# Two graph layers on one core: transposes of the norms through VectorE and DRAM, output products spread over two steps

## The chip, the cores and the metric

The kernel runs on one core of a Trainium2 chip. A core has five engines that run side by side, each through its own instructions in order: TensorE (matmuls; PE in the profile, with its weight loads as PEld), VectorE (DVE), ScalarE (ACT), GpSimd (POOL) and SyncE (SP), which here only issues the transfers (DMA) between DRAM and the on-chip memory SBUF. TensorE writes its results into PSUM[...]. The metric is the device time of one execution in microseconds.

## The reference, cut to what matters

x holds 64 batches of 256 rows of 512 float32 values; `adj` is one 256x256 mask for all. Two layers, each on a normalised and clipped copy of x:

```python
# layer 0: one head; W is 512x256, a is 2x256
h = relu(layernorm(x)) @ W
e = leaky_relu(h @ a[0] + (h @ a[1]).T, 0.2) + NEG * (1 - adj)
x = x + concat([softmax(e) @ h, h])
# layer 1: 8 heads of 64
n = relu(layernorm(x))
q, k, v = n @ Wq.T + bq, n @ Wk.T + bk, n @ Wv.T + bv
attn = softmax(where(adj == 0, -inf, q @ k.T / 8))      # for each head
x = x + (attn @ v) @ Wo.T + bo
```

## The kernel before

The batches are taken in 32 groups of two (`GB = 2`; `GT = 4` tiles of 128 rows in a group). Three groups are under way at once. While the attention of group g runs (four **steps**: two batches, each in two `quad`s of four heads), the q, k, v products of group g+1 (`project`, 21 pieces) and the first layer of group g+2 (`first_layer`) are cut into pieces and strung between. Each product with a 512x512 weight is done by a scheme with seven half-size products in place of eight (`seven`, `operand_sums`), which needs sums of the operand's blocks first.

A matmul needs the normalised x with its columns on the partitions. `norm_T` normalises a tile of 128 rows on VectorE and turns it on TensorE, by four transposes of 128x128 into a PSUM bank; ScalarE clips it on the way out:

```python
def norm_T(src, mv, name):
    ve = small.tile([P, GT], F32, tag="ve", ...)
    nc.vector.tensor_scalar(ve, mv[:, :, 1], EPS, None, op0=ALU.add)
    nc.gpsimd.tensor_tensor(rstd, ve, rexp, op=ALU.pow)      # all four tiles at once
    def normed(t):
        xn[t] = att.tile([P, D], F32, tag="xn", ..., bufs=2)
        latest[0] = nc.vector.tensor_scalar(                 # line 354
            xn[t], src[:, t, :], mv[:, t, 0:1], rstd[:, t : t + 1],
            op0=ALU.subtract, op1=ALU.mult).ins.name
    def put(t, dst):
        if t + 1 < GT:
            normed(t + 1)
        pt = mm(f"pt{name}_{t}").rearrange("p (c t) -> p c t", c=HP)
        for c in range(HP):
            transpose(pt[:, c, :], xn[t][:, c * P : (c + 1) * P], ident)
        nc.scalar.activation(dst, pt, AF.Relu)
    normed(0)
    return put
```

`mm(...)` takes the next of five rotating PSUM banks, `held_bank(n, ...)` one of three fixed ones. `matmul` and `transpose` keep TensorE's instructions in the order of the program.

```python
def first_layer(g):                       # each yield ends a piece
    for t in range(GT): stats(mv, xt, t, ...)           # bn_stats, bn_aggr on VectorE
    put = norm_T(xt, mv, f"0_{g}")
    yield GAP
    ...                                   # per tile: put, then ph = hT @ W (H), x += H on GpSimd
    ...                                   # pn, e: scores of the first layer
    for r in range(GT):                   # po = e @ H, times 1/sum, added to x
        ...
        stats(mv, xt, r, f"1_{g}")
        yield
    put = norm_T(xt, mv, f"1_{g}")
    yield GAP
    for t in range(GT): put(t, hT[:, :, t * P : (t + 1) * P]); ...
    operand_sums(quads, sums)             # four GpSimd instructions
    for t in range(GT): nc.gpsimd.tensor_add(xt[:, t, :], xt[:, t, :], b_out)

def scores(g, b, quad):                   # a step's first half
    ...                                   # sc = k.T q; p = exp(sc) on ScalarE
    nc.vector.tensor_mul(pair, pair, maskT...)           # line 573
    nc.gpsimd.tensor_add(ps[...], pair[:, :, 0, :], pair[:, :, 1, :])

def weigh(g, b, quad, p, ps):             # one step later
    pr = mm(f"pr_{name}")...
    ...                                   # pr = v.T p, 16 matmuls
    total = held_bank(2, f"total_{name}")[:, :N]
    for j in range(QH):                   # sums over the rows
        matmul(total[j * S : (j + 1) * S, :], ones[:, :S], ps[:, j, :], start=True, stop=True)
    nc.vector.reciprocal(r, total)                       # line 604
    nc.vector.tensor_mul(oT[:, 2 * quad : 2 * quad + 2, :], pr, r...)

def outputs(g, b):                        # seven pieces, after a batch's second weighing
    operand_sums(quads, sums)             # four GpSimd instructions (o_sums)
    first = held_bank(2, f"py1_{g}_{b}")[:, : D // 2]
    product(first, 1, True)
    add(0, 0, first)                      # VectorE: x += product, line 628
    yield
    ...

steps = ("uosuoosuosoosuos", "uusususususu", "uosoosuosoosuos", "uusususususu")
for g in range(NG):
    for step, parts in enumerate(steps):
        if waiting is not None:
            weigh(*waiting)
            if waiting[2] == NQ - 1: late = outputs(*waiting[:2])
        waiting = (g, b, quad, *scores(g, b, quad))
        for part in parts:                # u: project(g+1), o: outputs, s: first_layer(g+2)
            ...
```

Beside it stand `last_bias`, a small product at the start whose four columns are built on VectorE in one buffer, and `judge`, some small matmuls that bound the sizes of the scores.

Of the kernel before, what the change touches and what calls it, by code (L numbers as in the profile page):

```python
# [14 lines left out]
P = 128  # L15
# [8 lines left out]
LARGEST_VALUE = 1e6  # L24

# [17 lines left out]
def bounded(  # L43
# [23 lines left out]
    nc = tc.nc  # L67
    B, N, D = x.shape
# [17 lines left out]
    psum = ctx.enter_context(tc.tile_pool(name="psum", bufs=1, space=bass.MemoryType.PSUM))  # L86

# [15 lines left out]


# [13 lines left out]
    xg = x.rearrange("(g b) (t p) d -> g p (b t) d", b=GB, p=P)  # L118
    og = out.rearrange("(g b) (t p) d -> g p (b t) d", b=GB, p=P)
# [3 lines left out]
    def load(g):  # L123
        xs[g] = big.tile([P, GT, D], F32, tag="x", name=f"x{g}", bufs=4)
        nc.sync.dma_start(xs[g], xg[g])

    load(0)
# [16 lines left out]
    for c in range(HP):  # L144
        for s in range(2):
            nc.vector.scalar_tensor_tensor(
                prod, w0_sb[:, c, 2:], 1.0, a_b[:, s, :], op0=ALU.mult, op1=ALU.mult,
                accum_out=w0_sb[:, c, s : s + 1],
            )
    edge = att.tile([P, NT, N], F32, tag="e", name="edge")  # L150
    nc.vector.tensor_scalar(edge, adj_i, 0.0, None, op0=ALU.not_equal)
# [6 lines left out]
    nc.vector.tensor_copy(maskT, pt)  # L158

    nc.vector.reduce_max(bad[:, 0, :], edge, axis=AX.X)  # L160
    nc.vector.tensor_scalar(bad[:, 0, :], bad[:, 0, :], 0.0, None, op0=ALU.is_equal)
    nc.vector.tensor_tensor(edge, edge, adj_i, op=ALU.not_equal)
    nc.vector.reduce_max(bad[:, 1, :], edge, axis=AX.X)

    load(1)
    load(2)

# [28 lines left out]
    rexp = const.tile([P, GT], F32, name="rexp")  # L196
    nc.gpsimd.memset(rexp, -0.5)
    ones = const.tile([P, P], F32, name="ones")
    nc.gpsimd.memset(ones, 1.0)

    def weight_sums(name):
        w = w_sb[name]
        first = nc.vector.tensor_sub(w[:, :, T3, :], w[:, :, W22, :], w[:, :, W12, :])
        after(first, latest[0])
        nc.vector.tensor_sub(w[:, :, T1, :], w[:, :, W12, :], w[:, :, W11, :])
        nc.vector.tensor_sub(w[:, :, T2, :], w[:, :, W22, :], w[:, :, T1, :])
        nc.vector.tensor_sub(w[:, :, T4, :], w[:, :, W21, :], w[:, :, T2, :])

    def last_bias():


        pb = mm("pb")
        for q in range(NQ):
            for half in range(2):
                b = small.tile([P, P], F32, tag="power", name=f"bv_{q}_{half}", bufs=1)
                nc.vector.tensor_scalar(b, ones, bv_col[:, half, q : q + 1], None, op0=ALU.mult)
                matmul(
                    pb, b, w_sb["o"][:, half, 2 * q : 2 * q + 2, :],
                    start=(q == 0 and half == 0), stop=(q == NQ - 1 and half == 1),
                )  # L220
        nc.vector.tensor_add(b_out, pb, b_out)


    def judge():
# [5 lines left out]
        nc.vector.memset(part, 0.0)  # L230
        junk = att.tile([P, D], F32, tag="junk", name="junk", bufs=1)

        def squares(col, *srcs):
            sums = small.tile([P, HP], F32, tag="sums", name=f"sums{col}", bufs=2)
            for i, src in enumerate(srcs):
                nc.scalar.activation(
                    junk[:, : src.free_size()], src, AF.Square, accum_out=sums[:, i : i + 1]
                )
            nc.vector.reduce_sum(part[:, col : col + 1], sums[:, : len(srcs)], axis=AX.X)

        for s in range(2):
            squares(s, w0_sb[:, :, s])
        squares(2, *[w0_sb[:, c, 2:] for c in range(HP)])
        wv = att.tile([P, HP, D // HP], F32, tag="block", name="wv_block", bufs=1)
        sums = small.tile([P, HP], F32, tag="sums", name="sums3", bufs=2)
        for c in range(HP):
            nc.sync.dma_start(
                wv, wvT[:, c * P : (c + 1) * P].rearrange("(c p) o -> p c o", p=P)
            )
            nc.scalar.activation(  # L250
                junk, wv.rearrange("p c o -> p (c o)"), AF.Square, accum_out=sums[:, c : c + 1]
            )
        nc.vector.reduce_sum(part[:, 3:4], sums, axis=AX.X)
        squares(4, bcol["q"])
        squares(5, bcol["k"])
        squares(6, bv_col.rearrange("p h q -> p (h q)"))
        nc.vector.reduce_max(part[:, 7:8], bad.rearrange("p a t -> p (a t)"), axis=AX.X)
        yield
        heads = const.tile([P, P], F32, name="heads")
        nc.vector.memset(heads, 0.0)  # L260
        for j in range(2):
            nc.vector.memset(heads[j * DH : (j + 1) * DH, j * DH : (j + 1) * DH], 1.0)
        rowsq = const.tile([P, 2, HP], F32, name="rowsq")
        for n, (name, src) in enumerate((("q", wqT), ("k", wkT))):
            for hp in range(HP):
                w = att.tile([P, HP, P], F32, tag="block", name=f"w{name}_block{hp}", bufs=1)
                nc.sync.dma_start(
                    w, src[:, hp * P : (hp + 1) * P].rearrange("(c p) o -> p c o", p=P)
                )
                yield  # L270
                gram = mm(f"gram_{name}{hp}")[:, :P]
                for c in range(HP):
                    matmul(
                        gram, w[:, c, :], w[:, c, :], start=(c == 0), stop=(c == HP - 1)
                    )
                a = small.tile([P, P], F32, tag="power", name=f"power_{name}{hp}_0", bufs=1)
                nc.vector.tensor_mul(a, gram, heads)
                yield
                for i in range(3):
                    square = mm(f"square_{name}{hp}_{i}")[:, :P]  # L280
                    matmul(square, a, a, start=True, stop=True)
                    if i < 2:
                        a = small.tile(
                            [P, P], F32, tag="power", name=f"power_{name}{hp}_{i + 1}", bufs=1
                        )
                        nc.vector.tensor_copy(a, square)
                    else:
                        nc.scalar.activation(
                            junk[:, :P], square, AF.Square, accum_out=rowsq[:, n, hp : hp + 1]
                        )  # L290
                    yield
        nc.vector.reduce_sum(part[:, 8:10], rowsq, axis=AX.X)
# [3 lines left out]
        nc.vector.tensor_scalar(norm, total, 1e-30, None, op0=ALU.add)  # L296
        power = const.tile([P, 10], F32, name="power")
        nc.gpsimd.memset(power, 0.5)
        nc.gpsimd.memset(power[:, 7:8], 1.0)
        nc.gpsimd.memset(power[:, 8:10], 1.0 / 32)  # L300
        nc.gpsimd.tensor_tensor(norm, norm, power, op=ALU.pow)
# [5 lines left out]
        nc.vector.tensor_add(test[:, 0:1], norm[:, 0:1], norm[:, 1:2])  # L307
        nc.vector.tensor_scalar(
            test[:, 0:1], test[:, 0:1], root / LARGEST_SCORE, None, op0=ALU.mult
        )  # L310
        nc.vector.tensor_scalar(side, norm[:, 8:10], root, None, op0=ALU.mult)
        nc.vector.tensor_add(side, side, norm[:, 4:6])
        nc.vector.tensor_mul(test[:, 1:2], side[:, 0:1], side[:, 1:2])
        nc.vector.tensor_scalar(
            test[:, 1:2], test[:, 1:2], scale / LARGEST_SCORE, None, op0=ALU.mult
        )
        nc.vector.tensor_scalar(
            test[:, 2:3], norm[:, 2:3], root / LARGEST_VALUE, None, op0=ALU.mult
        )
        nc.vector.scalar_tensor_tensor(  # L320
            test[:, 3:4], norm[:, 3:4], root, norm[:, 6:7], op0=ALU.mult, op1=ALU.add
        )
        nc.vector.tensor_scalar(
            test[:, 3:4], test[:, 3:4], 1.0 / LARGEST_VALUE, None, op0=ALU.mult
        )
        nc.vector.tensor_scalar(test[:, 4:5], norm[:, 7:8], 2.0, None, op0=ALU.mult)
        nc.vector.tensor_scalar(test, test, 1.0, None, op0=ALU.is_le)
        held = const.tile([P, 1], F32, name="held")
        nc.vector.tensor_reduce(held, test, axis=AX.X, op=ALU.min)
        nc.vector.tensor_scalar(wrong, held[0:1, :], -1.0, 1.0, op0=ALU.mult, op1=ALU.add)  # L330
# [5 lines left out]
    GAP = "gap"  # L336

    def stats(mv, src, t, name):
        st = small.tile([P, 6], F32, tag="st", name=f"st{name}_{t}")
        nc.vector.bn_stats(st, src[:, t, :])  # L340
        nc.vector.bn_aggr(mv[:, t, :], st)

    def norm_T(src, mv, name):


        ve = small.tile([P, GT], F32, tag="ve", name=f"ve{name}")
        nc.vector.tensor_scalar(ve, mv[:, :, 1], EPS, None, op0=ALU.add)
        rstd = small.tile([P, GT], F32, tag="rstd", name=f"rstd{name}")
        nc.gpsimd.tensor_tensor(rstd, ve, rexp, op=ALU.pow)
        xn = {}  # L350

        def normed(t):
            xn[t] = att.tile([P, D], F32, tag="xn", name=f"xn{name}_{t}", bufs=2)
            latest[0] = nc.vector.tensor_scalar(  # L354
                xn[t], src[:, t, :], mv[:, t, 0:1], rstd[:, t : t + 1],
                op0=ALU.subtract, op1=ALU.mult,
            ).ins.name

        def put(t, dst):
            if t + 1 < GT:  # L360
                normed(t + 1)
# [712 lines left out]
```

## Time and profile before

| | |
|---|---|
| time, median of three | 2699.87 us |
| profiled span | 2697.3 us |
| mean granted TensorE clock | 0.993 |
| busy: PE, DVE, ACT, POOL | 2620.4, 1669.7, 835.9, 1230.0 us |
| moved by DMA | 78.49 MB, 29 GB/s in the mean |

In the profile "L113" is the line of a helper that records every matmul, so matmuls are told apart by the tiles they write: `pq`, `pk`, `pv` projections, `sc` scores, `pr` and `total` weighing, `py` output products, `ph`, `pn`, `po` first layer, `pt` transposes of the norms. A group of instructions is shown with its busy time, the mean duration of one, and the idle time of its engine ahead of it with what ended it. Matmuls overlap one another, so the mean duration of one is more than the time between two.

### The profile page before, as it was taken

The page shows a single profiled execution, that of the slowest core. Times are in us where ns is not written, and L with a number is a line of the kernel's source. Part 1 is how long each engine was busy: PE and PEld are TensorE (multiplying, and loading weights), DVE is VectorE, ACT ScalarE, POOL GpSimd, SP SyncE. Part 2 cuts the span into 40 slices and gives each one's busy share as a digit, 9 for nine tenths or more (in the row PEclk, how much of TensorE's full clock was granted, in tenths as well). Part 3 has the DMA queues.
Part 4 walks back from the last instruction along what each step waited for, and adds up shares of the span by engine and source line. Part 5 has one row for each costly group of instructions (what it writes and reads, how often), then busy time and mean ns, then how long its engine had stood idle before and what let it go on. Part 6 is the DMA issues. An engine that isn't in the chain of part 4 may idle for free.

```text
span 2697.3 us, 41512 instructions
## 1 busy us (share of the span) xinstructions
PE 2620.4 (97%) x17150; PEld 2118.8 (79%) x17150; DVE 1669.7 (62%) x2558; ACT 835.9 (31%) x1771; POOL 1230.0 (46%) x1004
## 2 busy tenths in 40 slices
PE   5999999999999999999999999999999999999997
PEld 3888888878888887887788888788878878878874
DVE  5666566666557665566665576665576656666544
ACT  2333232333332333323333323333333333233321
POOL 2353355443445443545434454435455335445343
PEclk8999999999999999999999999999999999999998
DMA  5000101000001010000000000000000000000000
GB/s 164 1 12 32 36 24 36 13 32 32 28 32 36 9 36 32 24 32 9 32 32 24 32 32 9 32 32 24 32 32 9 32 32 24 32 17 23 17 16 25
DMA packets 45890, 78.49 MB, mean 29 GB/s; under 512 B 3712, under 2 KB 10624, under 8 KB 45696
## 3 DMA queue, kind: packets, MB, share of 16 engines
q1 hardware_dynamic: 45696, 75.77, 8.1%
q8 instruction: 137, 2.24, 0.3%
q14 instruction: 57, 0.47, 0.1%
HBM read 42.21 MB, written 33.55 MB: 28 GB/s over the span
## 4 chain that ended last, share of the span: by engine, by line
PE 89%; DVE 8%; POOL 1%; issue 1%; DMA 0%; ACT 0%; DVEq 0%
PE pq L113 15%; PE pv L113 14%; PE py L113 13%; PE pk L113 13%; PE pr L113 9%; PE ph L113 8%; PE sc L113 7%; PE po L113 4%; PE pt L116 4%; DVE p L573 3%; DVE r L604 2%; PE total L113 2%; DVE k L544 1%; DVE oT L605 1%; PE pn L116 1%
## 5 line engine op out<-in xcount | busy, mean ns | idle before, releaser
L573 DVE TENSOR_TENSOR p<-p,maskT 128x1024 f32<-128x1024 f32 x256 | 398.6, 1588 | 0.6 <-ACT p L572 0.5
L572 ACT ACTIVATE p<-sc 128x512 f32<-128x512 f32 x512 | 264.4, 602 | 380.9 <-PE sc L113 380.9
L574 POOL TENSOR_TENSOR ps<-p 128x512 f32<-128x512 f32 x256 | 366.2, 1447 | 0.0
L628 DVE TENSOR_TENSOR x<-py,x 128x256 f32<-128x256 f32 x448 | 187.6, 419 | 272.8 <-PE py L113 266.9
L604 DVE RECIPROCAL r<-total 128x256 f32<-128x256 f32 x128 | 224.5, 1754 | 194.6 <-PE total L113 194.6
L113 PE MATMUL py<-wo_sb,o_sums 128*128 128x256 f32 x1024 | 266.5, 384 | 26.4 <-DVE x L628 21.6
L420 POOL TENSOR_TENSOR x<-H,x 128x256 f32<-128x256 f32 x128 | 87.7, 685 | 443.0 <-ACT H L419 441.9
L113 PE MATMUL pr<-p,v 128*32 128x256 f32 x4096 | 251.8, 385 | 5.8 <-DVE p L573 5.8
L113 PE MATMUL sc<-q,k 64*128 64x256 f32 x2048 | 255.7, 389 | 0.0
L113 PE MATMUL pq<-sums,wq_sb 128*128 128x256 f32 x1024 | 246.7, 384 | 4.2 <-POOL sums L377 3.7
L113 PE MATMUL ph<-w_sb,hT 128*128 128x258 f32 x1024 | 246.1, 383 | 0.0
L113 PE MATMUL pk<-sums,wk_sb 128*128 128x256 f32 x1024 | 244.8, 382 | 0.0
L113 PE MATMUL pv<-wv_sb,sums 128*128 128x256 f32 x1024 | 242.0, 379 | 0.1
L113 PEld LDWEIGHTS sc<-q,k 64*128 64x128 f32 x2048 | 187.2, 186 | 69.7 <-issue 52.6
L113 PEld LDWEIGHTS py<-wo_sb,o_sums 128*128 128x128 f32 x1024 | 191.2, 192 | 62.9 <-POOL o_sums L377 37.6
L365 ACT ACTIVATE hT<-pt 128x512 f32<-128x512 f32 x256 | 153.1, 599 | 266.0 <-PE pt L116 265.7
L354 DVE TENSOR_SCALAR xn<-x,mv,rstd 128x512 f32<-128x512 f32 x256 | 225.8, 893 | 9.5 <-PE pt L116 4.9
L376 POOL TENSOR_TENSOR o_sums<-oT 128x256 f32<-128x256 f32 x64 | 106.2, 1660 | 262.6 <-DVE oT L605 262.6
L113 PEld LDWEIGHTS pq<-sums,wq_sb 128*128 128x128 f32 x1024 | 190.1, 191 | 39.1 <-issue 9.9
L113 PEld LDWEIGHTS ph<-w_sb,hT 128*128 128x128 f32 x1024 | 195.7, 192 | 28.6
L113 PEld LDWEIGHTS pk<-sums,wk_sb 128*128 128x128 f32 x1024 | 189.3, 190 | 33.9 <-issue 9.9
L113 PEld LDWEIGHTS pr<-p,v 128*32 128x32 f32 x4096 | 121.1, 110 | 112.2 <-issue 39.7
(145 smaller groups left out, 4054.4 us busy)
## 6 DMA issues: line engine op xcount, KB each, us to landing
x<-in_x_dram SPq DMA_DIRECT2D x32, 1024.0 KB, 5.5
out_dram<-x SPq DMA_DIRECT2D x64, 512.0 KB, 2.8
wq_sb<-in_L_gnn_Wq_dram SPq DMA_DIRECT2D x2, 512.0 KB, 11.7
wk_sb<-in_L_gnn_Wk_dram SPq DMA_DIRECT2D x2, 512.0 KB, 12.4
wv_sb<-in_L_gnn_Wv_dram SPq DMA_DIRECT2D x2, 512.0 KB, 11.4
wo_sb<-in_L_gnn_Wo_dram SPq DMA_DIRECT2D x8, 128.0 KB, 3.3
wv_block<-in_L_gnn_Wv_dram SPq DMA_DIRECT2D x4, 256.0 KB, 3.0
wq_block<-in_L_gnn_Wq_dram SPq DMA_DIRECT2D x4, 256.0 KB, 2.9
```

Source lines behind the costliest of these rows:

```text
L113: in_order(nc.tensor.matmul(*args, **kwargs))
L116: in_order(nc.tensor.transpose(*args))
L354: latest[0] = nc.vector.tensor_scalar(xn[t], src[:, t, :], mv[:, t, 0:1], rstd[:, t : t + 1], op0=ALU.subtract, op1=ALU.mult,).ins.name
L365: nc.scalar.activation(dst, pt, AF.Relu)
L376: nc.gpsimd.tensor_add(sums[:, 0], a21, a22)
L420: nc.gpsimd.tensor_add(xt[:, t, F1:], H[:, t, 2 : F1 + 2], xt[:, t, F1:])
L544: nc.vector.tensor_add(part(1, 1), first, p7)
L572: nc.scalar.activation(pair[:, j], sc[j], AF.Exp, scale=scale)
L573: nc.vector.tensor_mul(pair, pair, maskT[:, None, :, :].to_broadcast([P, 2, NT, N]))
L574: nc.gpsimd.tensor_add(ps[:, 2 * i : 2 * i + 2, :], pair[:, :, 0, :], pair[:, :, 1, :])
L604: nc.vector.reciprocal(r, total)
L628: nc.vector.tensor_add(to, out, to)
```

## The change

It takes the transposes of the norms off TensorE. VectorE turns the 32x32 blocks of a normalised tile; a transfer writes a batch to DRAM, and four transfers read it back so that block (j, i) comes to where block (i, j) was; ScalarE clips it on the way to its place. Only the first group is still turned on TensorE, as nothing stands beside it to hide the way through DRAM. Around this the pieces are rearranged:

- the norm of x goes one batch at a time, in pieces of its own (`n`), a step or more ahead of the first layer that uses it; x is loaded by batch;
- the output products of a batch are spread over two steps, and the sums of their operands move from GpSimd to VectorE;
- the rows' sums run ahead of the weighing, in a rotating bank;
- the addition of the last bias to x is put a step later; the columns of `last_bias` are built on GpSimd, each in a place of its own; `judge` works on the weights already in SBUF and runs at the start;
- `not_sooner` ties an instruction to the one recorded before it on its engine, so that it isn't put ahead.

```diff
+    def not_sooner(engine, operation, *args, **kwargs):
+        last = engine.last
+        after(getattr(engine, operation)(*args, **kwargs), last)
...
+    def norm_T(src, mv, name, by_pe):
+        def norm(b):
+            vector.tensor_scalar(ve, mv[:, tiles, 1], EPS, None, op0=ALU.add)
+            gpsimd.tensor_tensor(rstd, ve, rexp, op=ALU.pow)
+            for t in range(NT):
+                xn[r] = att.tile([P, D], F32, tag="xn", ..., bufs=2)
+                not_sooner(vector, "tensor_scalar", xn[r], src[r], mv[:, r, 0:1], rstd[:, t : t + 1],
+                    op0=ALU.subtract, op1=ALU.mult)
+        def turn(b):
+            if by_pe:
+                ...                       # as before, on TensorE
+                return
+            xt = att.tile([P, J, HP, NT, S], F32, tag="xt", ..., bufs=1)
+            moved = att.tile([P, J, HP, NT, S], F32, tag="moved", ...)
+            passed = dram.tile([P, J, HP * NT * S], F32, tag="passed", ...)
+            for t in tiles:
+                not_sooner(vector, "transpose",
+                    xt[:, :, :, t % NT, :], xn[t].rearrange("p (c j a) -> p j c a", j=J, a=S))
+                turned[t] = moved[:, :, :, t % NT, :].rearrange("p i c n -> p c i n")
+            nc.sync.dma_start(passed, xt.rearrange("p j c t n -> p j (c t n)"))
+            for j in range(J):
+                nc.sync.dma_start(
+                    moved[j * S : (j + 1) * S].rearrange("a i c t n -> a i (c t n)"),
+                    passed.rearrange("(i a) j e -> j a i e", a=S)[j])
+        def put(b, dst):
+            ...                           # two relus on ScalarE, by not_sooner
...
+    def first_norm(g):                    # six pieces: norm, turn, norm, turn, put, put
...
             stats(mv, xt, r, f"1_{g}")
+            if r == 2:
+                norm(0)
+            elif r == 3:
+                turn(0)
             yield
+        norm(1)
+        yield
+        turn(1)
+        yield
+        put(0, hT[:, :, :N])
+        yield
+        put(1, hT[:, :, N:])
...
+        total = mm(f"total_{name}")[:, :N]
+        ...                               # total and its reciprocal, now ahead of pr
         pr = mm(f"pr_{name}").rearrange("p (h n) -> p h n", h=2)
-        total = held_bank(2, f"total_{name}")[:, :N]
...
+        if quad == NQ - 1:
+            operand_sums(vector, quads, sums)
...
-    steps = ("uosuoosuosoosuos", "uusususususu", "uosoosuosoosuos", "uusususususu")
+    steps = ("Suuunuonuonuuo", "Sssnuosuosouso", "Sususuososuos", "sSsuuousouounuonsu")
...                                       # S: scores, n: a piece of first_norm(g+2), later (g+3)
+            if step == 0 and g + 1 < NG:
+                residual(g + 1)           # x += b_out
```

## The prediction

> **What bounds the kernel now.** I read four views in this order: busy time by engine with the chain that ended last, the waits of the matmul engine, its busy time by stretch, and the costliest groups.
>
> ```profile
> PE 2620.4 (97%) x17150; PEld 2118.8 (79%) x17150; DVE 1669.7 (62%) x2558; ACT 835.9 (31%) x1771; POOL 1230.0 (46%) x1004
> ...
> PE 89%; DVE 8%; POOL 1%; issue 1%; DMA 0%; ACT 0%; DVEq 0%
> ```
>
> PE is busy for 97% of the span and makes up 89% of the chain. So almost every microsecond on PE is a microsecond of the result, and the other engines matter only where PE waits for them. The waits of PE between 140 and 2494 us are few:
>
> ```profile
> PE py L113 <- DVE x L628: 19.9, 25, 1.0
> PE pt L116 <- DVE xn L354: 2.9, 1, 2.9
> PE py L113 <- DVE part L292: 0.6, 1, 0.6
> ```
>
> The columns are the total, the count and the longest. PE's only repeated wait is for VectorE to add an output product into x: 25 times about 0.8 us. By stretch, the first, a long middle and the last (the columns are length, then PE, PEld, DVE, ACT, POOL busy):
>
> ```profile
> 0.00:67.50 67.50, 35.86 (x129) 25.51 (x130) 38.23 (x93) 17.21 (x44) 18.73 (x28) 0.87 0.51 164
> ...
> 202.50:1300.00 1097.50, 1087.86 (x7184) 885.69 (x7182) 678.73 (x1050) 346.05 (x736) 506.15 (x410) 1.00 0.08 29
> ...
> 2630.00:2697.30 67.30, 49.85 (x365) 33.56 (x363) 33.54 (x41) 8.85 (x17) 25.00 (x19) 0.88 0.07 25
> ```
>
> PE idles 31.6 us at the start, 17.5 us at the end, and 9.6 us in 1097 us of the middle. In the timeline one group of two batches (from the first scores matmul of one to that of the next, 1263.1 to 1344.6) takes 81.5 us, with PE busy for 80.65. The groups that the change touches:
>
> ```profile
> L116 PE MATMUL pt<-ident,xn 128*128 128x128 f32 x1024 | 156.2, 276 | 10.6 <-DVE xn L354 10.6
> ...
> L573 DVE TENSOR_TENSOR p<-p,maskT 128x1024 f32<-128x1024 f32 x256 | 398.6, 1588 | 0.6 <-ACT p L572 0.5
> L354 DVE TENSOR_SCALAR xn<-x,mv,rstd 128x512 f32<-128x512 f32 x256 | 225.8, 893 | 9.5 <-PE pt L116 4.9 <-POOL rstd L349 3.6 <-issue 0.2
> L604 DVE RECIPROCAL r<-total 128x256 f32<-128x256 f32 x128 | 224.5, 1754 | 194.6 <-PE total L113 194.6
> ...
> L376 POOL TENSOR_TENSOR o_sums<-oT 128x256 f32<-128x256 f32 x64 | 106.2, 1660 | 262.6 <-DVE oT L605 262.6
> L349 POOL TENSOR_TENSOR rstd<-ve,rexp 128x4 f32<-128x4 f32 x64 | 71.5, 1118 | 160.9 <-DVE mv L341 129.9 <-DVE ve L347 28.0
> ```
>
> The 276 ns of a transpose is a latency, not its cost: matmuls overlap. In the timeline four transposes begin at 1333.46 and the next product at 1333.89, so four cost 0.43 us, **108 ns each**. By the same reading a projection piece (8 instructions) costs 1.73 us, an output piece (4) 0.86, a first-layer piece of four matmuls 1.74, a weighing (pr and total) with its scores about 4.4.
>
> [...] no VectorE transpose stands in this trace. [...] here a 128x512 pass out of PSUM takes 0.68 to 0.69 us. My estimate is 0.65 us. [...] the mask product takes 1.22 us where GpSimd is quiet and 1.59 in the mean; the o_sums take 0.72 us in the quiet end and 1.66 in the mean. [...]
>
> **The change part by part.**
>
> *PE transposes.* Group 0 keeps them. The other 31 groups lose 2 norms x 4 tiles x 4 = 32 transposes each: 992 x 0.108 = **107 us** off PE, all on the path. That is 3.46 us per group.
>
> *VectorE.* Added: 31 x 8 = 248 block transposes x 0.65 = 161 us; the o_sums, 256 instructions of 128x256 at about 0.40 us (half of a 128x512 pass of 0.69, and some fixed part) = 102 us; twice as many variance instructions, 64 x 0.2 = 13. Removed: about 60 us of contention, an estimate, as GpSimd loses the 350 us of its o_sums. 1670 + 161 + 102 + 13 - 60 = about 1890 us, 73% of a span of 2590. ACT does the same number of relus as before. GpSimd: 1230 - 350 + 64 more powers x 1.12 = about 950.
>
> *Bursts.* The mean hides the steps, so I count a group's four steps, PE against VectorE, with the norm's wait for the power on GpSimd (about 1.2 us) counted as VectorE time, since order is now pinned. Step 0: PE 4.4 + 7 x 1.73 + 3 x 0.86 = 19.1; VectorE 2.4 (reciprocal, weighing) + 1.6 (sums) + 3.2 (masks) + 2.1 (adds of products) + 4.9 (norm of x with its statistics) + 1.3 + 1.3 = 16.8. Step 1: PE 20.5, VectorE 11. Step 2: PE 4.4 + 4 x 1.73 + 4 x 0.87 + 3 x 0.86 = 17.4; VectorE 4.0 + 3.2 + 4 x 1.5 (rows of the first layer with statistics) + 3.2 (norm) + 1.3 + 1.3 + 1.4 = 20.4. Step 3: PE 20.0, VectorE 2.4 + 3.2 + 3.2 + 1.3 + 2.1 + 1.7 + 4.9 + 1.3 = 20.1. PE sums to 77.0, which agrees with 81.5 - 3.46 - 0.8 of idle. VectorE sums to 68: it fits, but falls some 3 us behind in step 2 and recovers only in the next step 0 and 1. Five rotating PSUM banks hide part of that. I put new waits at 1 us per group: **+30 us**.
>
> *Order of a weighing and output products.* The sums of rows run before the weighing, so the 1.75 us reciprocal overlaps the 1.86 us of pr instead of following it, and total no longer takes the bank that the first output product needs. With seven output pieces spread over two steps, the 20 us wait of py for x should go: **-20 us**. At the end of the kernel the last group has nothing but weighings, scores and output pieces; its four steps took about 13, 11, 13 and 11 us. Spread, each should take 9 or so, which is set by exp, mask and the sum on GpSimd: 10 us less.
>
> *Start.* bv columns move to GpSimd with a buffer each, which ends the alternation of VectorE and PE around 45 to 52 us; but the norm of group 1 comes earlier: **-5 us** net. The small matmuls of the bound check move to the start, equal in number.
>
> *Transfers.* A batch goes out as 512 KB and comes back as four of 128 KB: 124 x 1 MB = 130 MB more, on top of 78 MB, about 80 GB/s over the span; the first slice moved 164. The page gives 2.8 us for 512 KB out and 2.9 us for 256 KB in, so a round trip is about 2.8 + 4 issues x 0.4 + 2.5 = 7 us. The tightest place is step 2's last piece to step 3's relu: between them PE has 2.5 + 1.9 + 3.5 + 0.9 + 1.7 = 10.5 us. It fits, with about 1 us left once VectorE's lag is counted.
>
> Sum: 2700 - 107 - 20 - 10 - 5 + 30 = 2588, rounded to **2590**.
>
> **The rivals.**
> *VectorE becomes the bound in steps 2 and 3.* For it: its work is now pinned in order with a wait on GpSimd inside it, and 20 us of work stand in both steps. Against it: 68 of 77 us over a group, and masks are needed a whole step later. If the lag of 3 us per group lands on PE, 2590 + 60 = 2650; if transposes cost 1.3 us rather than 0.65, 2700.
> *The round trip comes late.* Then ACT stops at a relu, since its order is pinned too, the exps and PSUM evacuations behind it are late, and PE waits for banks. For it: 1 us of slack at the tightest place, and one queue in order. Against it: a DMA share of 0.08 and about 15 us of distance at the other three places. Late by 2 us per group, it makes 2650.
> *GpSimd's relief is worth more.* With 280 us less on GpSimd the masks and norms get faster, the lag doesn't build up, and no new wait is left: 2555.
>
> **Range and chances.** 2550 is no new wait at all; 2665 is 3.4 us of new waits per group, nearly all that the transposes gave. Staying within 2% (above 2646) needs 2.8 us or more per group, one of the first two rivals in full; slower by 2% needs both and more. Faster 0.80, within 2% 0.14, slower 0.06.
>
> **What would show it.** PE busy about 107 us less and 992 fewer matmuls; the transposes on VectorE at 0.6 to 0.7 us; VectorE near 73%; GpSimd near 950; no py wait for x. Against me would speak: repeated waits of PE for VectorE in steps 2 and 3; ACT idle before a relu with the DMA named as releaser; transposes over 1 us; mask products no shorter than 1.5 us.

## The result, and the profile after

The changed kernel takes 2660.95 us (median of 2659.71 to 2661.95) beside 2700.72 for the kernel before in the same series: a ratio of 0.9853, 95% interval 0.9836 to 0.987. The gain is 40 us. The prediction had been 110.

The page of the kernel after, busy time by engine and the chain that ended last:

```profile
PE 2546.2 (96%) x16158; PEld 2035.1 (77%) x16158; DVE 1892.7 (71%) x3103; ACT 829.5 (31%) x1759; POOL 993.7 (37%) x816
...
PE 53%; DVE 28%; POOL 9%; issue 7%; ACT 2%; DMA 1%; SPq 0%; DVEq 0%; ACTq 0%; POOLq 0%
```

The instruction counts are as planned: 992 matmul instructions fewer on PE, VectorE at 71%, GpSimd at 994 us. The second line is the chain. PE made up 89% of it before and makes up 53% now, with 28% on VectorE; hardly any of it is transfers (DMA 1%). The shares alone don't say what is wrong: in the fastest kernel below, 76 us faster, they are still 57% and 32%.

PE's waits in the middle (202.5 to 2450 us; total, count, longest), kernel after:

```profile
PE pq L135 <- POOL sums L35: 47.0, 28, 1.7
PE py L135 <- DVE x L35: 8.7, 28, 0.3
```

In the same stretch of the kernel before, py waited for x for 18.2 us in 23 places and nothing waited for `sums`. Now the third product of each q projection waits 1.7 us in every group for GpSimd's sums of the operand, and py still waits a little.

How PE's idle time is spread (length of the stretch less PE's busy time in it):

| stretch | before | after |
|---|---|---|
| start, 0 to 202.5 us | 34.7 | 40.0 |
| middle, 202.5 to 2450 us | 21.7 | 55.7 |
| end, from 2450 us | 20.5 | 15.9 |
| whole | 76.9 | 111.6 |
| PE busy, whole | 2620.4 | 2546.2 |

The table closes: busy time falls by 74.2, idle time grows by 34.7, and the span is 39.5 shorter (2697.3 to 2657.8). But busy time should have fallen by 107. The groups show where most of the rest is. Kernel after (busy, mean ns of one, idle ahead of it):

```profile
L135 PE MATMUL sc<-q,k 64*128 64x256 f32 x2048 | 286.5, 393 | 0.0
L135 PEld LDWEIGHTS sc<-q,k 64*128 64x128 f32 x2048 | 203.9, 186 | 83.8 <-issue 52.6 <-DVE r L35 11.4
L35 DVE TENSOR_TENSOR p<-p,maskT 128x1024 f32<-128x1024 f32 x256 | 434.1, 1717 | 48.3 <-ACT p L35 48.1
L35 DVE STREAM_TRANSPOSE xt<-xn 128x512 f32<-128x512 f32 x248 | 159.7, 681 | 0.0
L35 ACT ACTIVATE hT<-moved 128x512 f32<-128x512 f32 x248 | 142.2, 625 | 0.8 <-DMA moved<-passed 0.8
L35 POOL TENSOR_TENSOR sums<-sums,hT 128x512 f32<-128x512 f32 x32 | 69.9, 2186 | 0.0
```

The same two groups in the kernel before:

```profile
L113 PE MATMUL sc<-q,k 64*128 64x256 f32 x2048 | 255.7, 389 | 0.0
...
L377 POOL TENSOR_TENSOR sums<-sums,hT 128x512 f32<-128x512 f32 x32 | 41.8, 1307 | 0.0
```

Read them in this order. The scores matmuls are the same 2048 instructions, yet they cover 30.8 us more of PE's time with nearly the same mean (393 and 389 ns) and 0.0 us of idle time ahead of them: a gap inside such a run shows here as a longer run (2.68 us in the timeline below, 2.00 in steps 1 and 3), not as idle time. The weight loads (PEld) name what is waited for there: the reciprocal `r` (11.4 us of their idle time). Some 11 of the 30.8 us come with the rearrangement and not with the way through VectorE: the scores take 266.8 us in run e4 below, which has the one without the other. The mask products got slower (1588 to 1717 ns), and one kind of sum on GpSimd went from 1307 to 2186 ns. The block transpose takes 681 ns. And the relu on `moved` waits for its transfer for 0.8 us in the whole kernel: where ScalarE gets to the relu, the data are there.

One group's step 0 in the timeline of the kernel after (start, length, engine, operation; in brackets the idle time of the engine ahead of it and what ended it):

```profile
1321.90 1.73 SPq L404 DMA_DIRECT2D moved<-passed  x4
...
1327.25 0.64 PE L135 MATMUL total<-ps,ones 128*32 128x256 f32 x8
1327.35 0.59 ACT L35 COPY v<-pv 128x512 f32<-128x512 f32 x1 [5.87 <-PE pv L135]
...
1328.10 1.30 DVE L35 STREAM_TRANSPOSE xt<-xn 128x512 f32<-128x512 f32 x2
1329.32 1.72 DVE L35 RECIPROCAL r<-total 128x256 f32<-128x256 f32 x1
...
1329.54 2.68 PE L135 MATMUL sc<-q,k 64*128 64x256 f32 x16
...
1330.77 0.60 ACT L35 ACTIVATE p<-sc 128x512 f32<-128x512 f32 x1 [2.83 <-PE sc L135]
...
1331.26 1.14 ACT L35 ACTIVATE hT<-moved 128x512 f32<-128x512 f32 x2
...
1332.15 3.72 PE L135 MATMUL pq<-hT,wq_sb 128*128 128x256 f32 x16
...
1332.48 2.82 POOL L35 TENSOR_TENSOR sums<-hT 128x512 f32<-128x512 f32 x2 [5.33 <-ACT hT L35]
...
1334.09 4.49 DVE L35 TENSOR_TENSOR p<-p,maskT 128x1024 f32<-128x1024 f32 x2
...
1335.26 2.24 POOL L35 TENSOR_TENSOR sums<-sums,hT 128x512 f32<-128x512 f32 x1
1337.55 2.64 PE L135 MATMUL pq<-sums,wq_sb 128*128 128x256 f32 x11 [1.68 <-POOL sums L35]
```

Two things go wrong here, and neither is a lack of capacity.

First, the transfers back are all issued by 1323.6 and take 2.9 us each (the page's median), so by my estimate from these two the data lie in SBUF by about 1326.5. The relu that takes them runs at 1331.26. ScalarE was idle for 2.83 us of that: in its program the relu stands *behind* the copy of v and the first exp, and that exp waits for scores. The source has the relu ahead of both. `not_sooner` kept the relu behind what was recorded before it, but nothing kept the copy and the exp, recorded later, from being put ahead of the relu. So GpSimd, idle for 5.33 us, begins the sums late; they fall on the mask products, both grow (two masks 4.49 us, a sum 2.24; 2.35 and 1.26 in run e3 below), and PE waits 1.68 us.

Second, the reciprocal can begin at 1327.9, when total is there, but stands behind the norm and two block transposes and begins at 1329.32. `total` now lies in one of the five rotating banks, and the fourth scores tile, five allocations later (total, pr, sc, sc, sc, then sc), needs it back. The scores matmuls take 2.68 us in place of the 2.00 that they take in steps 1 and 3. In step 2 they take 2.38, as the reciprocal stands there behind the first layer's two passes over e.

### The profile page after: what moved, and what is told of

Its sections match the earlier page's. It is cut to its first block, busy times and chain, and to the rows that moved or that the text cites. A ratio compares the mean times of both kernels' runs of the same rounds, so it can differ in the third digit from the quotient of the medians.

```text
span 2657.8 us, 41200 instructions
## 1 busy us (share of the span) xinstructions
PE 2546.2 (96%) x16158; PEld 2035.1 (77%) x16158; DVE 1892.7 (71%) x3103; ACT 829.5 (31%) x1759; POOL 993.7 (37%) x816
## 3 DMA queue, kind: packets, MB, share of 16 engines
q8 instruction: 129, 2.11, 0.3%
## 4 chain that ended last, share of the span: by engine, by line
PE 53%; DVE 28%; POOL 9%; issue 7%; ACT 2%; DMA 1%; SPq 0%; DVEq 0%; ACTq 0%; POOLq 0%
PE pq L135 11%; PE py L135 10%; PE ph L135 8%; PE pv L135 7%; PE pk L135 7%; POOL sums L35 6%; PE pr L135 4%; DVE r L35 4%; PE sc L135 4%; DVE x L35 4%; DVE xn L35 3%; DVE xt L35 3%; DVE p L35 3%; POOL rstd L35 3%; DVE st L35 2%
## 5 line engine op out<-in xcount | busy, mean ns | idle before, releaser
L35 DVE TENSOR_TENSOR p<-p,maskT 128x1024 f32<-128x1024 f32 x256 | 434.1, 1717 | 48.3 <-ACT p L35 48.1
L35 ACT ACTIVATE p<-sc 128x512 f32<-128x512 f32 x512 | 267.1, 602 | 382.3 <-PE sc L135 382.3
L135 PE MATMUL pq<-sums,wq_sb 128*128 128x256 f32 x1024 | 244.5, 388 | 59.2 <-POOL sums L35 59.2
L35 POOL TENSOR_TENSOR rstd<-ve,rexp 128x2 f32<-128x2 f32 x128 | 120.7, 943 | 449.9 <-DVE ve L35 444.5
L135 PE MATMUL sc<-q,k 64*128 64x256 f32 x2048 | 286.5, 393 | 0.0
L135 PEld LDWEIGHTS sc<-q,k 64*128 64x128 f32 x2048 | 203.9, 186 | 83.8 <-issue 52.6
L35 DVE TENSOR_SCALAR xn<-x,mv,rstd 128x512 f32<-128x512 f32 x256 | 179.0, 730 | 109.1 <-POOL rstd L35 107.9
L135 PE MATMUL pr<-p,v 128*32 128x256 f32 x4096 | 245.5, 379 | 0.0
L35 POOL TENSOR_TENSOR x<-x,b_out 128x512 f32<-128x512 f32 x128 | 198.2, 1558 | 53.1 <-DVE xn L35 31.8
L135 PEld LDWEIGHTS pv<-wv_sb,sums 128*128 128x128 f32 x1024 | 194.5, 190 | 26.6 <-DVE v L35 0.3
L135 PE MATMUL py<-wo_sb,oT 128*128 128x256 f32 x768 | 200.2, 384 | 12.0 <-DVE x L35 12.0
```

Source lines behind the costliest of these rows:

```text
L35: instruction = getattr(self.engine, operation)(*args, **kwargs)
L135: in_order(nc.tensor.matmul(*args, **kwargs))
```

## The experiments

Two theories. **Order**: the work fits, but instructions stand in the wrong place in queues that run in order, so that sums and masks, reciprocals and scores meet. **Load**: VectorE has too much to do in a step, or the way through DRAM is late; then no reordering helps. All ratios are to the kernel before; every edit is to the kernel after unless said otherwise.

### e1: the sum that is needed first goes first

GpSimd's order was sums[0], sums[2], sums[1]; the waiting product needs sums[1].

```diff
 engine.tensor_sub(sums[:, 1], sums[:, 0], a11)
-engine.tensor_sub(sums[:, 2], a11, a21)
+not_sooner(engine, "tensor_sub", sums[:, 2], a11, a21)      # on GpSimd only
```

> The changed kernel, but on GpSimd the second sum (which the third projection product reads) runs before the third one instead of after it. Theory 'order': PE waits 1.7 us per group for that sum only because another sum of 1.4 us runs first; the wait of pq for sums falls from 59 to under 15 us and the time from 2661 to about 2615 (2605 to 2630). Rival 'VectorE is full': the wait goes, but PE waits as long for VectorE a little later: 2650 or more. Rival 'transfers late': the sums' input comes too late for any order to help, pq still waits over 40 us: 2650 or more.

Measured: 2653.0 us, ratio 0.9831 (0.9815 to 0.9848), 8 us better than the change, with intervals that overlap. The wait for `sums` fell from 59.2 to 7.1 us over the whole kernel, but a new one came: pq for q on VectorE, 41.1 us in 29 places. The masks still took 4.49 us a pair, and the q that frees a bank stood behind them. So taking away the named wait moved it one step on; what is late and slow stayed late and slow. By what was written beforehand this outcome spoke for VectorE being full. It doesn't settle it, as the masks on VectorE were still slowed by GpSimd's sums; e3 takes that away.

### e2: the reciprocal ahead of the norm

The norm's piece goes behind step 0's scores, so that the reciprocal no longer stands behind it (one norm piece fewer in the start's order too).

```diff
-steps = ("Suuunuonuonuuo", "Sssnuosuosouso", "Sususuososuos", "sSsuuousouounuonsu")
+steps = ("Snuuunuonuonuuo", "Sssnuosuosouso", "Sususuososuos", "sSsuuousouounuosu")
```

> The changed kernel, but the last piece of the norm of x in a group's step 3 (its block transposes) runs in the next step 0 behind the scores, so that the reciprocal of the rows' sums stands ahead of the transposes on VectorE. Theory 'order': the scores matmuls of step 0 take 2.0 instead of 2.7 us, since the bank of total comes free before the fourth of them needs it; the wait of pq for sums stays or grows a little; 2645 (2635 to 2655). Rival 'VectorE is full': no gain, 2655 to 2670, with the stretch moved to another matmul.

Measured: 2703.36 us, ratio 1.0013 (1.0006 to 1.002), 42 us worse than the change. The scores did get shorter (286.5 to 267.1 us; 2.00 us in step 0), as expected, but 2645 had been expected in all. The sums still met the masks, and PE's wait for them grew from 1.68 to 3.02 us per group (47.0 to 84.6 us in the middle). And then something new came, in the stretches of that kernel around one such wait (length, then PE, PEld, DVE, ACT, POOL busy, granted clock, DMA share, GB/s):

```profile
1355.50:1358.50 3.00, 0.03 (x1) 0.00 (x0) 3.00 (x3) 0.00 (x0) 3.00 (x2) 0.89 0.00 0
1358.50:1362.00 3.50, 3.45 (x8) 2.82 (x9) 2.50 (x7) 0.00 (x0) 3.42 (x3) 0.50 0.37 150
1362.00:1365.10 3.10, 3.10 (x9) 2.44 (x9) 1.00 (x2) 0.84 (x2) 0.96 (x2) 0.57 0.63 169
```

PE stands for 3 us, and for the next 6.6 us its clock is about halved (0.50 and 0.57): 16 matmuls take 6.72 us in place of 3.72. That is the worst group; most take 5.2 or 3.72. The 42 us are thus 37.6 of longer waits, 23.9 of slower pq matmuls (their group went from 244.5 to 268.4), less 19.4 of scores. Mending one of the two faults made the other worse.

### e3: the relu ahead of the copy and the exp

`not_sooner` pins the last copies of v, and the first exp of a group, behind the relus in ScalarE's order.

```diff
 def take(to, bank, half):
+    if name == "v" and half == 1:
+        not_sooner(scalar, "copy", to, bank)
+        return
...
-    scalar.activation(pair[:, j], sc[j], AF.Exp, scale=scale)
+    if b == quad == i == j == 0:
+        not_sooner(scalar, "activation", pair[:, j], sc[j], AF.Exp, scale=scale)
+    else:
+        scalar.activation(pair[:, j], sc[j], AF.Exp, scale=scale)
```

> The changed kernel, but on ScalarE the last relus of a group's norm stand ahead of the last copy of v and of the first exp of the next step, instead of behind them. Theory 'order': their data landed at about 1326.5 while they ran at 1331.3, so the sums start some 3.5 us sooner and the wait of pq for sums is gone: 2610 (2600 to 2625), without any transfer being faster. Rival 'transfers late': ScalarE now stands and waits for the transfer, the exps come later and nothing is gained: 2655 to 2680, with ScalarE idle before hT and a DMA named. Rival 'VectorE is full': 2645 or more.

Measured: 2606.8 us, ratio 0.9663 (0.9647 to 0.9679), **54 us better than the change** with not one instruction more or less. The timeline of the same step in this kernel:

```profile
1302.51 1.15 ACT L35 ACTIVATE hT<-moved 128x512 f32<-128x512 f32 x2 [5.74 <-DMA moved<-passed]
1303.11 1.00 DVE L35 TENSOR_SCALAR xn<-x,mv,rstd 128x512 f32<-128x512 f32 x2 [0.60 <-POOL rstd L35]
1303.17 0.64 PE L135 MATMUL total<-ps,ones 128*32 128x256 f32 x8
...
1303.74 2.74 POOL L35 TENSOR_TENSOR sums<-hT 128x512 f32<-128x512 f32 x2 [0.67 <-ACT hT L35]
...
1306.45 1.26 POOL L35 TENSOR_TENSOR sums<-sums,hT 128x512 f32<-128x512 f32 x1
...
1310.18 2.35 DVE L35 TENSOR_TENSOR p<-p,maskT 128x1024 f32<-128x1024 f32 x2
```

The relu now runs 0.7 us ahead of total, where it ran 4.0 us after it. ScalarE is seen to wait for the transfer (5.74 us of idle time ends with it). In the middle that costs PE nothing; at the start it does once, when a v product waits 7.3 us for ScalarE. The sums are over before the masks begin; a pair of masks takes 2.35 us in place of 4.49, a sum 1.26 in place of 2.24, and PE's wait for sums is gone. What is left is the scores, still 286.7 us, with 9.8 us of open waiting for `r`. VectorE has all its instructions still. This decides for order in the larger of the two faults.

### e4: the rearrangement alone

Every norm is turned on TensorE again, by four transposes a tile when it is needed; no block transposes, no way through DRAM. All the rest of the change stays.

```diff
-xn[r] = att.tile([P, D], F32, tag="xn", name=f"xn{name}_{r}", bufs=2)
+xn[r] = att.tile([P, D], F32, tag="xn", name=f"xn{name}_{r}", bufs=8)
...                                       # turn(b): empty; in put(b, dst), per tile:
+pt = mm(f"pt{name}_{b}_{t}").rearrange("p (c n) -> p c n", c=HP)
+for c in range(HP):
+    transpose(pt[:, c, :], xn[b * NT + t][:, c * P : (c + 1) * P], ident)
+scalar.activation(dst[:, :, t * P : (t + 1) * P], pt, AF.Relu)
```

> The changed kernel with all its rearrangement, but every norm is transposed on TensorE again, when its relu is due (no block transposes on VectorE, no way through DRAM). Theory 'order': the rearrangement by itself is worth little; PE gets its 107 us back and loses only a part of its new waits, 2715 (2690 to 2745). Rival 'the way through VectorE and DRAM makes all new waits': the waits of about 90 us vanish with it, 2660 to 2680, the time of the changed kernel.

Measured: 2655.99 us, ratio 0.9839 (0.9822 to 0.9855). So the rearrangement alone is worth 43 us, and moving the transposes on top of it, as the change did it, gave nothing more (it is 5 us slower, which the intervals don't tell apart). The middle stretch of this kernel:

```profile
202.50:2450.00 2247.50, 2247.50 (x14790) 1835.12 (x14789) 1454.26 (x2416) 716.93 (x1503) 831.68 (x694) 1.00 0.08 27
```

By the page PE isn't idle at all for 2247 us (the scores' 2.38 us in step 2 hide 0.38 of waiting here too). From its first exp of one group to that of the next a group takes 80.8 us here; less 32 transposes of 108 ns (3.46 us) that is 77.3 us, which a group without them could take. The changed kernel's group takes 80.5. So **3.2 us of new waiting per group** eat the 3.46 us that the transposes gave. I had expected this run to be slow, and it wasn't: the rearranged order is good for TensorE's transposes, and its fault appears only with the VectorE way.

### f1: both mends together (e2 and e3)

> The relus of the norm first (2607) and the reciprocal first together. With the reciprocal first alone the scores of step 0 took 2.0 us as expected, but the relus and the sums then met the masks and cost more than was won. If that meeting is the whole cause of the loss, then with the relus first nothing is lost and the 20 us of stretched scores come on top: 2587 (2578 to 2595), clock back at 0.99. If the order of the transposes itself costs (VectorE too full), 2605 to 2640.

Measured: 2594.9 us, ratio 0.9609 (0.9593 to 0.9625), 12 us better than e3. The edit that cost 42 us alone gains 12 once the sums no longer meet the masks. Scores take 275.5 us. In step 0 they take 2.46 us, less than the change's 2.68, but not the 2.00 of e2:

```profile
1300.27 1.97 DVE L35 TENSOR_SCALAR xn<-x,mv,rstd 128x512 f32<-128x512 f32 x2 [0.60 <-POOL rstd L35]
...
1300.65 2.72 POOL L35 TENSOR_TENSOR sums<-hT 128x512 f32<-128x512 f32 x2 [0.42 <-ACT hT L35]
...
1302.63 2.46 PE L135 MATMUL sc<-q,k 64*128 64x256 f32 x16
```

With the relus early, GpSimd's sums fall on the two norms. These take 1.97 us in place of 1.00, and the reciprocal, which stands behind them, is late again. The meeting has moved from the masks to the norms, where it costs less. In step 2 the scores take 2.38 us as in e4.

### f2: e3 without the way through DRAM

ScalarE reads `xt` directly. This leaves out the permutation of the 32x32 blocks, so each matmul works on wrongly placed blocks; number and shape of all compute instructions stay, and the transfers go.

```diff
-xt = att.tile([P, J, HP, NT, S], F32, tag="xt", name=f"xt{name}_{b}", bufs=1)
+xt = att.tile([P, J, HP, NT, S], F32, tag="xt", name=f"xt{name}_{b}")
-turned[t] = moved[:, :, :, t % NT, :].rearrange("p i c n -> p c i n")
+turned[t] = xt[:, :, :, t % NT, :].rearrange("p i c n -> p c i n")
-nc.sync.dma_start(passed, ...)           # and the four transfers back
```

> The kernel with the relus first, with the way through DRAM left out: ScalarE reads the block-transposed tile itself, so blocks are not permuted and the output is another one. Theory 'order': transfers end in time, 2606 (2600 to 2610), equal to that with them, but for some us at the start. Rival 'transfers late': their waits are still hidden in the other engines' waits, 2560 to 2590.

Measured: 2620.49 us, ratio 0.9702 (0.9686 to 0.9719), 14 us *slower* than with the transfers. PE's largest wait in the middle of this kernel:

```profile
PE sc L135 <- DVE r L35: 26.9, 28, 1.0
```

An equal time had been expected. Without the delay of the transfers the relus and sums come earlier and meet the norms on VectorE in every group (`xn` 833 ns in place of 762), and the reciprocal behind these is later still. So the transfers, 130 MB of them, don't set the time; when things meet does.

### f3: e3 with the sums of output operands back on GpSimd

```diff
-operand_sums(vector, quads, sums)        # o_sums
+operand_sums(gpsimd, quads, sums)
```

> The kernel with the relus first, with the operand sums of the output products back on GpSimd. VectorE is relieved of 135 us (71% to 66%), GpSimd gets some 300 back. [...] GpSimd has sums, o_sums and row sums in one stretch of step 0, which contend with the masks; the sums come too late for the third projection product or the o_sums for the third output product: 2640 (2620 to 2670), masks longer. Rival 'VectorE is full': relief of VectorE takes away the last waits, 2580 to 2600.

Measured: 2620.44 us, ratio 0.9704 (0.9688 to 0.972). VectorE's share falls from 71% to 68%, and the kernel is 14 us slower than e3: the scores' waiting for `r` grew from 9.8 to 20.7 us. If VectorE's load alone were the bound, this would have helped. It isn't a clean test, though: GpSimd gets 255 us of work more, and the norms on VectorE become slower (762 to 800 ns). The waits for late sums that had been expected didn't come; the wait is for `r`. The move of these sums to VectorE is a good part of the change.

### f4 and g0: two mends at the start

f4 is f1 with the squares of the bound check (`judge`) written to SBUF in place of rotating PSUM banks, for which a k product waited 5.5 us once. g0 is f4 with the second norm of group 1 turned on TensorE too, so that ScalarE no longer waits for its transfer at the start, where a v product waited 7.1 us.

```diff
-to = mm(f"squares{col}_{i}")[:, : src.free_size()]                          # f4
+to = room[:, :HP, :].rearrange("p a b -> p (a b)")[:, : src.free_size()]
...
-norm, turn, put = norm_T(xt, mv, f"1_{g}", g == 0)                          # g0
+norm, turn, put = norm_T(xt, mv, f"1_{g}", g <= 1)
```

> Relus and reciprocal first, and the squares of the bound check written to SBUF instead of into rotating PSUM banks. At the start PE waited 5.5 us once for a bank that these squares held: 5 us less than the kernel with both (2 to 7), so about 2582; nothing else moves.

> Relus and reciprocal first, squares in SBUF, and the second norm of group 1 turned on TensorE too (16 transposes more). With the relus first, ScalarE waited some 7 us once at the start for a transfer and PE with it: that wait goes, 1.7 us of transposes come; 5 us less than 2590, so 2585 (2581 to 2592).

Measured: f4 2590.3 us, ratio 0.9589 (0.9573 to 0.9605); g0 2585.0 us, ratio **0.9573 (0.9557 to 0.9589)**. Each gives about 5 us, which is near the noise, but both waits are gone from the traces. g0 computes all that the kernel before does and is the best of all here: 76 us better than the change, 115 better than before. A group takes 78.35 us in it.

### g3: the first layer's scores work behind step 2's scores

An attempt on what is left in step 2: the pieces with pn and e go behind the reciprocal (an edit of g0).

```diff
-steps = ("Snuuunuonuonuuo", "Sssnuosuosouso", "Sususuososuos", "sSsuuousouounuosu")
+steps = ("Snuuunuonuonuuo", "Sssnuosuosouo", "Ssuuoussusosos", "sSsuuousouounuosu")
```

> As the kernel before it in this list, but the first layer's scores (pn, e) move from the end of step 1 to behind the scores of step 2, so that the reciprocal of step 2 stands ahead of the four passes over e on VectorE; the rows of the first layer then fall into the second half of step 2. If stretched scores are simply a late reciprocal, they fall from 276 to 266 us and the time to 2575 (2570 to 2582). If VectorE is full in step 2, its lag of 3 us now reaches step 3 with the norm and the transfers behind it, and the time rises: 2600 to 2640.

Measured: 2696.69 us, ratio 0.999 (0.9983 to 0.9997): 112 us lost against g0. The timeline of this kernel's step 2:

```profile
1310.18 3.44 DVE L35 SCALAR_TENSOR_TENSOR e<-e 128x512 f32<-128x512 f32 x2
...
1313.65 0.63 ACT L35 ACTIVATE e<-e 128x512 f32<-128x512 f32 x1 [1.05 <-DVE e L35]
1314.19 0.46 ACT L35 ACTIVATE kept_k<-pk,bk_sb 128x256 f32<-128x256 f32 x1
1314.70 1.99 PE L135 MATMUL pk<-hT,wk_sb 128*128 128x256 f32 x8 [2.31 <-ACT kept_k L35]
```

Step 2's scores do take 2.00 us now, as was hoped. But VectorE's passes over e stand behind the reciprocal, the weighing and the masks. ScalarE, in order, waits for them with the exp of e; the evacuation of k's bank stands behind that, and PE waits 2.31 us in each of 27 groups, 62 of the 112 us. In the same stretch py's wait for x grows from 8.9 to 19.1 us, and scores wait 14.7 us for `r`, now in step 3. So here VectorE's burst does reach PE, as the first rival of the prediction had it, for the larger part through an unrelated evacuation that stands behind an exp that waits.

## Why the prediction was wrong

**The transposes (-107): right in the main.** 992 instructions are gone. Of the 3.46 us per group that they should free, g0 shows 2.45 in hand (a group of 78.35 beside 80.8 in e4); the rest is the 1 us that stays open below. On VectorE a transpose takes 681 ns (650 by my estimate), VectorE is at 71% (73%), GpSimd at 994 us (950). That VectorE's total fits is in part luck: the sums of output operands took 135 us (102), and masks and norms together became 11 us shorter, not 60.

**Order of weighing and output products (-20), end (-10), start (-5): right as a sum, through e4.** e4 is 43 us faster than before where these terms make 35: in its idle time, 21.7 in the middle, 8.9 at the end and 6.9 at the start. In the changed kernel itself py's wait fell by only 9.5 us in the middle, the end gained 4.6, and the start *lost* 5.3: its first sums came 7.5 us late, and a k product waited 5.5 us for banks of the bound check, which the prediction had counted as "equal in number". f4 and g0 took 10 us off the start.

**New waits ("I put new waits at 1 us per group: +30 us"): this step failed.** Against e4 they are 3.2 us per group, over three times as much: 1.7 open wait for sums (47.0 us in 28 places), 0.3 wait for x (8.7), 0.6 scores stretched by the reciprocal (286.5 less e4's 266.8, over 31 groups), and some 0.6 that no row names. Part of this last is only how a gap is counted: two q products begin at 1332.15, and at 1.73 us each the third would begin at 1335.61, but it begins at 1337.55, 1.94 us late, where 1.68 are shown as idle. The whole sum closes: 2588, less 8 as the rearrangement gave 43 in place of 35, plus 69 (2.2 us in 31 groups), plus 12 at the start (PE idles 40.0 us there beside e4's 27.8), is 2661. The prediction got the 1 us from adding up engine times per step and seeing that 68 us of VectorE's work fit in 77 of PE's. That sum says whether there is room, not in which order an in-order engine takes things. Three sentences of it hid the faults:

- "since its order is pinned too", of ScalarE: it is pinned on one side only. `not_sooner` says behind what an instruction stands, and nothing about what is put ahead of it; that is how the copy and the exp came ahead of the relu.
- "The tightest place is step 2's last piece to step 3's relu ... It fits": I looked for data that come too late, and at the relu of a group's first batch, which runs in time (step 3, 1320.34). The late one is that of the second batch, which wasn't looked at. Its data came early; the relu was late, behind a copy and an exp. e3 mends just that and gains 54 us.
- "total no longer takes the bank that the first output product needs": true, but it now takes a rotating bank that the fourth scores tile needs, and I counted "five rotating PSUM banks" as relief. f1 mends about a third of this in step 0 (2.68 to 2.46 us) and takes the open waits for `r` away, for 12 us more.

**The mask products.** "about 60 us of contention" was to go with GpSimd's o_sums. This was an estimate that the trace before didn't show: no mask product in it ran beside an idle GpSimd, and the 1.22 us "where GpSimd is quiet" stood beside a sum into `o_sums`:

```profile
1328.56 1.02 POOL L349 TENSOR_TENSOR rstd<-ve,rexp 128x4 f32<-128x4 f32 x1 [4.37 <-DVE mv L341]
1329.16 1.22 DVE L573 TENSOR_TENSOR p<-p,maskT 128x1024 f32<-128x1024 f32 x1
1329.55 1.42 POOL L378 TENSOR_TENSOR o_sums<-oT 128x256 f32<-128x256 f32 x1
```

In the change masks went the other way, 1588 to 1717 ns, since the sums now fell on them; in e3 they are at 1474. That was the sign named beforehand against the prediction, and the first place to look. The norms did gain, from 893 to 730.

**The rivals.** "VectorE becomes the bound" named a time (2650) near the result, but for the wrong cause: e3 leaves all the load and gains 54 us, and f3 takes load off VectorE and is slower. "The round trip comes late" is ruled out by f2 and by 0.8 us of waiting for transfers. With the order mended, the kernel takes 2585 to 2595 us, the time that had been predicted: the change holds what was seen in it, but its own order gives most of it back. That the number is met so closely is luck in part, as the rearrangement gave 8 us more than was put and two fixes at the start gave 10.

**What stays open.** Some 1 us per group is left in g0 (78.35 against 77.3). About 0.45 of it are step 0's scores (2.46 us against 2.00 in e4), late through the meeting of sums and norms that f1 shows; 0.3 is py's wait for x (8.9 us in 28 places). No run took this meeting and that with the masks away together. The 0.38 us of step 2 are in e4 as well, so they are no part of this 1 us; g3 took them away and lost more elsewhere. That pinning the relu brought the sums out of the way of the masks, and that this and not the relu itself counts, is read from the two timelines; no run took the collision away while leaving the relu late.

## What to carry to other kernels

When work moves from the bounding engine to others, adding up their times isn't enough: write down, for each engine that runs in order, what stands directly ahead of each new instruction and what *that* waits for. In the profile, compare the time an instruction starts with the time its data were there; idle time of its engine in between (2.83 us on ScalarE here) points to a wrong place in the order. And when a PSUM tile moves to a rotating pool, count the allocations until its bank comes round: that wait can show as longer matmul runs (2.68 us in place of 2.00 here) and not as idle time. When an instruction is tied to its place, tie what must not pass it too.

## What the runs showed of the hardware

**In e2 a gap of 3 us cost clock in about every second group; in the changed kernel one of 1.7 us did in none.** Two groups in a row of e2's timeline, after waits of 3.02 and 3.03 us:

```profile
621.66 3.72 PE L135 MATMUL pq<-sums,wq_sb 128*128 128x256 f32 x16 [3.02 <-POOL sums L35]
702.84 5.21 PE L135 MATMUL pq<-sums,wq_sb 128*128 128x256 f32 x16 [3.03 <-POOL sums L35]
```

The same gap costs 1.5 us in one group and nothing in the next, in turn through most of the kernel: of 18 such groups in e2's timelines ten take 5.14 to 6.72 us and eight 3.72. In the slowest, the one shown under e2, the granted clock is 0.50 and then 0.57. In the changed kernel a gap of 1.68 us left the 16 matmuls behind it at 3.72 us in all 28 groups of the middle (1337.55, with a clock of 1.00 from 1337.5 to 1341.3). The length of the gap alone doesn't decide it: near the end of the kernel before, a gap of 2.11 us was followed once by twelve matmuls in 4.54 us at a mean clock of 0.66 from 2664 to 2669 us (2664.01) and once by twelve in 2.86 at 1.00 from 2641.8 to 2645 (2641.85). What else decides it, no run here shows.

**Some meetings of VectorE and GpSimd cost both.** A mask product of 1.18 us (two in 2.35 in e3) became 2.24 in the changed kernel, and a GpSimd sum of 1.26 us became 2.24 beside it; two norms of 1.00 us in all became 1.97 in f1. So this mask and this sum took nearly as long side by side (2.24) as one after the other (1.18 + 1.26 = 2.44). Not every meeting costs that. In the trace of the changed kernel the 68 mask products beside an idle GpSimd take 1.22 us in the median and the 60 beside `sums` 2.28, but of the 68 beside a sum into `ps` 38 take 1.22 and 30 take 2.29. Why some meetings cost and others don't, no run here shows.
